# Two changes of DMA layout and queue in a two-layer scan kernel: 8-KB runs for two groups' intermediate, and the last phase's output stores on one queue

## The chip, the cores and the metric

The kernel runs on one core of a Trainium2 chip. The metric is the device time of one execution in microseconds (us), lower is better. The engines are PE (matmul), DVE (vector), ACT (scalar), POOL (general purpose) and SP, which does nothing here but issue DMAs. Both SP and ACT issue DMAs, each on a queue of its own; the profile calls SP's queue q1 and ACT's q10. ACT also computes, and it works its list in order: while it issues a DMA, or waits to, it doesn't compute.

## The reference

The input x has 32 images of 48 channels, 64 rows and 128 columns (fp32). Each of two layers normalises x over 16 groups of channels, then runs four scans over the picture (down and up over the rows, right and left over the columns), and adds the result to x:

```python
def step(w, b):
    def f(carry, inp):
        nxt = inp + _conv1d(carry, w, b)   # 5 taps along the other axis, 48 -> 48 channels
        return (nxt, nxt)
    return f
...
x = x + _L0_conv_ref(_gn(x), ...)
x = x + _L1_conv_ref(_gn(x), ...)
```

Every step of a scan needs the one before it, so the 64 rows are walked down and up and the 128 columns right and left, one after the other.

## The kernel before

**Tiling.** The 32 images are four groups of 8 (`GB`). A step is nine 128-wide matmuls and three additions on DVE that put a row (or column) in place. The chain of these steps is the kernel; all else is arranged around it.

**Phases.** `PHASES` lists twelve: for each layer the rows of groups 0, 1, 2 and 3, then the columns of groups 0 and 1 together (pair 0) and of 2 and 3 (pair 1). Phases 6 to 9 are the rows of layer 1, of which 8 and 9 (`JOINED`) share steps with the phase before; phase 10 and phase 11 are its columns. Phase 11 is the last one.

**Units.** In a column phase the picture is cut into four quarters of its columns (j), and each quarter into six units of 128 partitions x 2048 numbers (8 KB on each partition, 1 MB in all). The scan to the left finishes the quarters in the order 3, 2, 1, 0. What follows for each unit in phase 11 is written in `plan_cols`: `load_residual` brings the layer's input for the unit from `mid`, on ACT's queue; `add_residual` adds it (on POOL); `permute_unit` brings the eight 256-wide parts into the order of the output (three copies on POOL, five on ACT); `store_result` sends it to the output. For quarter 0, which is ready only when the scan ends, `last_results` does the same with the addition on DVE and the copies on ACT, POOL and DVE (3, 3, 2). Six tiles take the residuals in turn: a tile is loaded again when its unit's stores have landed.

**The intermediate.** `mid` (`source[1]`, one tensor in DRAM for each group) holds layer 0's result. It is written in phases 4 and 5 by `keep_result`, unit by unit (on SP's queue), read row by row in phases 6 to 9 by `take_rows` (SP's queue, runs of 32 numbers, 128 bytes), and read again unit by unit in phases 10 and 11 by `load_residual`. `by_quarter` gives the row view, `by_unit` the unit view. Its layout is [quarter, line, partition, 256]: the eight 1-KB lines of one partition of a unit lie 384 KB apart.

**The stores.** The output's rows of a quarter are 32 numbers long, so every output store of a column phase moves 128-byte runs. A unit is stored in three or four pieces (`pieces`), because 48 channels don't divide 128 partitions: 384, 384 and 256 KB, or 128, 384, 384 and 128 KB. In phase 11 the pieces alternate between SP's queue and ACT's; in the other phases all are on SP's.

**What sets the order.** `at(t, ...)` puts every piece of work on an agenda with a time in steps; `in_order` ties the instructions of each engine to that order. SP's list in phase 11 also has the six reads that bring back the units of quarter 0 which were spilled to DRAM (`spill_unit`); the scan needs them when it comes to quarter 0.

Of the kernel before, what the change touches and what calls it, by code (L numbers as in the profile page):

```python
# [29 lines left out]
F32 = mybir.dt.float32  # L30
# [3 lines left out]
C = 48  # L34
# [8 lines left out]
E8 = 8  # L43
FULL = 128
NG = E8 * C // FULL
NQ = 4
# [31 lines left out]
def weight_runs():  # L78
# [24 lines left out]
PHASES = (  # L103
    ("rows", 0, 0),
    ("rows", 0, 1),
    ("rows", 0, 2),
    ("rows", 0, 3),
    ("cols", 0, 0),
    ("cols", 0, 1),
    ("rows", 1, 0),  # L110
    ("rows", 1, 1),
# [10 lines left out]
def kernel(  # L122
# [8 lines left out]
    nc = tc.nc  # L131
    B, _, H, W = x.shape
    NK = W // E8
    NH = H // E8
# [4 lines left out]
    LINE = E8 * RUN  # L139
    UNIT = NH * LINE  # L140
    SLOT = 2 * NG * UNIT
    HALF = H // 2
    NGRP = B // GB
# [11 lines left out]
    dram = ctx.enter_context(tc.tile_pool(name="dram", bufs=1, space=bass.MemoryType.DRAM))  # L155
# [35 lines left out]
    def kept(name):  # L191
# [3 lines left out]
            for g in range(NGRP)  # L195
        ]

    source = [
        [
            dram.tile([E8 * NQ, C, UNIT], F32, tag=f"xin{g}", name=f"xin{g}")  # L200
# [2 lines left out]
            for g in range(NGRP)  # L203
        ],
        [
            dram.tile([NQ, NH, E8 * C, LINE], F32, tag=f"mid{g}", name=f"mid{g}")
            for g in range(NGRP)
        ],
    ]
# [53 lines left out]
    def by_quarter(t, e, h0, h1, q):  # L263


        t = t[q].rearrange("a (i c) (e n) -> e c (a i) n", i=E8, e=E8)
        return t[e, :, h0:h1]

    def by_unit(t, o, j):


        at = [(o * FULL, 0, FULL)]
        if o == NG - 1:
            at = [(6 * C, 0, 2 * C), (5 * C + C // 3, 2 * C, FULL)]
        t = t[j].rearrange("a m n -> m a n")
        return [(t[r : r + p1 - p0], p0, p1) for r, p0, p1 in at]

    def by_line(t):
# [18 lines left out]
    def dma(dst, src, queue=None):  # L297
        (queue or nc.sync).dma_start(dst, src)
# [21 lines left out]
    def pieces(o):  # L320
        return [(e, c0, c1, p0) for e, c0, c1, g, p0 in PIECES if g == o]
# [444 lines left out]
    def take_rows(k, h0, h1, o):  # L766

        _, layer, g = PHASES[k]
        turned = h1 - h0 > E8 and place(k, h0) > place(k, h0 + E8)
        if turned:  # L770
            for h in range(h0, h1, E8):
                take_rows(k, h, h + E8, o)
            return
        view = rows_at(k, h0, h1)
        for e, c0, c1, p0 in pieces(o):
            here = view[p0 : p0 + c1 - c0, o]
            for q in range(NQ):
                dma(
                    here[:, :, q * RUN : (q + 1) * RUN],
                    by_quarter(source[layer][g], e, h0, h1, q)[c0:c1],  # L780
                )
# [50 lines left out]
    def load_residual(k, j, i, nat):  # L832
        _, layer, pair = PHASES[k]
        o, half = UNITS[i]
        t = source[layer][2 * pair + half]
        if layer:
            for there, p0, p1 in by_unit(t, o, j):
                dma(by_line(nat)[p0:p1], there, nc.scalar)
        else:
            for e, c0, c1, p0 in pieces(o):  # L840
                here = nat[p0 : p0 + c1 - c0]
                if pair or half:
                    dma(here, x_by_col(t, e, j)[c0:c1])
                else:
                    dma(by_line(here), natural_col(t, e, j)[c0:c1])
# [6 lines left out]
    def keep_result(k, j, i):  # L852
        _, layer, pair = PHASES[k]
        o, half = UNITS[i]
        for there, p0, p1 in by_unit(source[1][2 * pair + half], o, j):
            dma(there, by_line(quarter(k, j)[:, half, o])[p0:p1])
# [17 lines left out]
    def in_output(j, g, e):  # L874


        t = out[g * GB : (g + 1) * GB].rearrange("b c (a e) w -> e (c a) b w", e=E8)
        return t[e, :, :, j * WQ : (j + 1) * WQ]

    def store_result(k, j, i, perm):  # L880
        pair = PHASES[k][2]
        o, half = UNITS[i]
        for n, (e, c0, c1, p0) in enumerate(pieces(o)):
            dst = in_output(j, 2 * pair + half, e)[c0 * NH : c1 * NH]
            src = perm[p0 : p0 + c1 - c0].rearrange("p (a b n) -> p a b n", a=NH, b=GB)
            queue = nc.scalar if n % 2 and k == len(PHASES) - 1 else nc.sync
            dma(dst.rearrange("(c a) b n -> c a b n", a=NH), src, queue)

    def hold_result(j, i, perm):
        o, half = UNITS[i]  # L890
# [225 lines left out]
    def plan_cols(k, t0, prev):  # L1116
# [32 lines left out]
        for u, (t, j, i) in enumerate(direct):  # L1149
            nat = tiles[u % n]  # L1150
            o, half = UNITS[i]
            if u < n:
                at(left + 16, load_residual, k, j, i, nat)
            if layer == 0:
                if u >= n:
                    at(max(direct[u - n][0] + 3, t - 21), load_residual, k, j, i, nat)
                at(t, add_residual, k, j, i, nat)
                at(t + 4, keep_result, k, j, i)
                unit = quarter(k, j)[:, half, o]
                if half == 0:  # L1160
                    for b in range(GB):
                        at(t + 5 + b, stats[0].take, j, o, unit, b)
                else:
                    at(t + 1, stats[1].take, j, o, unit)
            else:

                at(t, add_residual, k, j, i, nat)
                at(t + 2.5, permute_unit, k, j, i, nat, (nc.gpsimd, nc.scalar, nc.scalar))
                if final or j not in HELD:
                    at(t + 4.5, store_result, k, j, i, nat)  # L1170
                else:
                    at(t + 4.5, hold_result, j, i, nat)
                if final and j == 1:
                    at(t + 4.7, load_residual, k, 0, i, last_tiles(k)[i])

                if u >= 2 and u - 2 + n < len(direct):
                    at(t + 4.6, load_residual, k, *direct[u - 2 + n][1:], tiles[(u - 2) % n])
# [17 lines left out]
    def last_results(k):  # L1195

        for i, nat in enumerate(last_tiles(k)):
            perm = (*(stage[:, n] for n in range(4)), *spare_tiles)[i]
            add_residual(k, 0, i, nat, nc.vector)
            permute_unit(k, 0, i, perm, (nc.scalar, nc.gpsimd, nc.vector))  # L1200
            store_result(k, 0, i, perm)
# [3 lines left out]
    for k, (kind, *_) in enumerate(PHASES):  # L1205
        n = (H if kind == "rows" else W) - 1
# [283 lines left out]
```

## Time and profile before

| | |
|---|---|
| three runs, us | 4108.45, 4110.68, 4172.64; median 4110.68 |
| the profiled execution | 4108.49 us, its span (first to last instruction) 4106.8 us |
| PE busy | 4012.3 us, 98% of the span, mean granted clock 0.991 |
| DVE, ACT, POOL busy | 2078.8, 1306.9, 789.0 us |
| DMA | 681.57 MB in 2253898 packets, of which 2008848 are under 512 B |
| SP's queue, ACT's queue | 595.36 MB and 80.77 MB |

How to read it: the page's first part gives busy time by engine; the table of windows gives the same for stretches of the span, with the share of time in which the 16 DMA engines had packets and the GB/s. Packets of two queues can overlap, so that share can pass 1. The timeline lists an engine's instructions in order, with "ACTq" or "SPq" for the issue of a DMA; the time of such a row is the time the issuing took, not the transfer's. In a row of the timeline the bracket says how long the engine stood idle before and what ended it. The page's own chain of what ended last is one instruction long here (0.54 us) and tells nothing.

### The profile page before, as it was taken

Reading aid. Unit: us, or ns where it says so; the run is one execution under the profiler, and the core shown is the slowest. Engines: PE = TensorE matmul, PEld = TensorE weight load, DVE = VectorE, ACT = ScalarE, POOL = GpSimd, SP = SyncE. Lnnn points to the kernel's source line nnn. Section 1 sums busy time; section 2 is a strip of 40 time slices with the busy share of each in tenths; the row PEclk is TensorE's granted clock in tenths of the full one; section 3 lists DMA queues with packets and bytes.
Section 4 is the critical chain, followed back from the end, with each engine's and each line's share of the span. In section 5 each row is a group of like instructions: output and inputs, shape, how many; then the busy total and the mean of one; then the engine's idle time right before and its main releaser. Section 6 shows DMA issues by size and latency. Waiting matters only on the chain. (4 is left out here: it accounts for less than half of the span.)

```text
span 4106.8 us, 85201 instructions
## 1 busy us (share of the span) xinstructions
PE 4012.3 (98%) x34360; PEld 3927.0 (96%) x34360; DVE 2078.8 (51%) x6137; ACT 1306.9 (32%) x2628; POOL 789.0 (19%) x672
## 2 busy tenths in 40 slices
PE   6999999999999999999999999999999999999994
PEld 5999999999999999999999998888999999999994
DVE  6454454544444567546655443333444444444444
ACT  4557466430000355003773633434000002300122
POOL 5631303100000243002411000000000025610353
PEclk9999999999999999999999999999999999999997
DMA  9898897967993499804996965666698039999799
GB/s 299 220 223 185 245 189 218 171 108 97 147 181 60 141 245 288 193 2 155 242 161 143 142 102 96 101 108 104 103 166 202 1 77 245 299 251 155 147 234 196
DMA packets 2253898, 681.57 MB, mean 166 GB/s; under 512 B 2008848, under 2 KB 2206656, under 8 KB 2231232
## 3 DMA queue, kind: packets, MB, share of 16 engines
q1 hardware_dynamic: 2117568, 595.36, 70.3%
q10 hardware_dynamic: 135936, 80.77, 8.2%
q8 instruction: 270, 4.42, 0.5%
q14 instruction: 124, 1.02, 0.1%
HBM read 399.11 MB, written 295.93 MB: 169 GB/s over the span
## 5 line engine op out<-in xcount | busy, mean ns | idle before, releaser
L850 POOL TENSOR_TENSOR arena<-arena 128x2048 f32<-128x2048 f32 x80 | 362.5, 4547 | 1714.3 <-PE step_00l L915 521.3
L790 ACT ACTIVATE arena<-arena,offsetr,scaler 128x128 f32<-128x128 f32 (+1 forms) x576 | 345.2, 688 | 348.8 <-DMA arena<-mid 322.5
L648 ACT ACTIVATE early<-arena 128x256 f32<-128x256 f32 x192 | 129.7, 676 | 837.0 <-POOL arena L850 830.6
L790 ACT ACTIVATE arena<-arena,offset,scale 128x256 f32<-128x256 f32 (+2 forms) x360 | 249.0, 787 | 91.8 <-DMA arena<-xin 81.6
L709 POOL COPY arena<-arena 128x256 f32<-128x256 f32 x340 | 201.0, 653 | 383.7 <-DMA arena<-in_x 230.2
L915 PE MATMUL step_01r<-arena,early 128*128 128x128 f32 x2286 | 249.8, 272 | 0.0
L915 PE MATMUL step_11r<-arena,early 128*128 128x128 f32 x2286 | 249.2, 272 | 0.0
L915 PEld LDWEIGHTS step_11r<-arena,early 128*128 128x128 f32 x2286 | 248.7, 184 | 0.4 <-DVE arena L929 0.3
L915 PEld LDWEIGHTS step_01r<-arena,early 128*128 128x128 f32 x2286 | 248.9, 184 | 0.2
L915 PE MATMUL step_00r<-arena,early 128*128 128x128 f32 x2286 | 248.8, 272 | 0.0
L915 PEld LDWEIGHTS step_00r<-arena,early 128*128 128x128 f32 x2286 | 248.5, 184 | 0.2 <-DVE arena L929 0.2
L915 PE MATMUL step_10l<-arena,wleft 128*128 128x128 f32 x2286 | 248.5, 272 | 0.0
L915 PE MATMUL step_11l<-arena,wleft 128*128 128x128 f32 x2286 | 248.5, 272 | 0.0
L915 PE MATMUL step_00l<-arena,wleft 128*128 128x128 f32 x2286 | 248.4, 272 | 0.0
L915 PE MATMUL step_01l<-arena,wleft 128*128 128x128 f32 x2286 | 248.4, 272 | 0.0
L915 PE MATMUL step_10r<-arena,early 128*128 128x128 f32 x2286 | 248.4, 272 | 0.0
L915 PEld LDWEIGHTS step_10l<-arena,wleft 128*128 128x128 f32 x2286 | 248.4, 184 | 0.0
L915 PEld LDWEIGHTS step_11l<-arena,wleft 128*128 128x128 f32 x2286 | 248.4, 184 | 0.0
L915 PEld LDWEIGHTS step_00l<-arena,wleft 128*128 128x128 f32 x2286 | 248.4, 184 | 0.0
L915 PEld LDWEIGHTS step_01l<-arena,wleft 128*128 128x128 f32 x2286 | 248.4, 184 | 0.0
L915 PEld LDWEIGHTS step_10r<-arena,early 128*128 128x128 f32 x2286 | 248.4, 184 | 0.0
L872 ACT COPY arena<-arena 128x256 f32<-128x256 f32 x172 | 99.6, 656 | 366.6 <-POOL arena L850 234.7
(545 smaller groups left out, 6870.1 us busy)
## 6 DMA issues: line engine op xcount, KB each, us to landing
xin<-arena SPq DMA_DIRECT2D x94, 512.0 KB, 4.5
arena<-in_x SPq DMA_DIRECT2D x18, 2048.0 KB, 10.5
upa<-arena SPq DMA_DIRECT2D x192, 192.0 KB, 3.8
arena<-upa SPq DMA_DIRECT2D x96, 384.0 KB, 9.9
arena<-xin SPq DMA_DIRECT2D x96, 384.0 KB, 10.6
upb<-arena SPq DMA_DIRECT2D x192, 192.0 KB, 3.9
arena<-upb SPq DMA_DIRECT2D x96, 384.0 KB, 10.9
arena<-xin SPq DMA_DIRECT2D x174, 192.0 KB, 4.2
```

The costliest lines, as they stand in the source:

```text
L648: nc.scalar.activation(junk[:, 0:n], view[:, b], AF.Identity, accum_out=self.sum[:, i, j : j + 1])
L709: copy(dst[:, r, q], src[:, r0 + r, q])
L790: nc.scalar.activation(args[0], args[0], AF.Identity, bias=args[2], scale=args[1])
L850: eng.tensor_tensor(unit, unit, nat, ALU.add)
L872: copy(by_w(perm)[:, a], src[:, a])
L915: nc.tensor.matmul(part(turn(whole(ps[o]))[0:m], -s), weights[:, i, at : at + m], part(turn(src(i)), s), start=seen[o] == 1, stop=seen[o] ...
```

## The change

1. For groups 2 and 3 (`by_partition`) the layout of `mid` becomes [quarter, partition, 2048]: the eight lines of a partition lie one behind the other, 8 KB in one run, and a unit of 128 partitions is 1 MB in one piece (for the third unit of a half, whose partitions are held in two parts, 768 and 256 KB). Unit writes (phase 5) and unit reads (phase 11) then move 8-KB runs in place of 1-KB ones. The row reads of phases 8 and 9 keep their 128-byte runs, in the same number of DMAs; from one channel to the next it is 8 KB where it was 1 KB. Groups 0 and 1 stay as they were.
2. In phase 11 all pieces of a unit's store are issued on SP's queue, in the same order and the same sizes; ACT's list there has the residual loads and its copies only.

```diff
+    def by_partition(g):
+
+        return g >= NGRP - 2
+
...
         [
-            dram.tile([NQ, NH, E8 * C, LINE], F32, tag=f"mid{g}", name=f"mid{g}")
+            dram.tile(
+                [NQ, E8 * C, UNIT] if by_partition(g) else [NQ, NH, E8 * C, LINE],
+                F32,
+                tag=f"mid{g}",
+                name=f"mid{g}",
+            )
             for g in range(NGRP)
         ],
...
     def by_quarter(t, e, h0, h1, q):
 
 
+        if len(t.shape) == 3:
+            t = t[q].rearrange("(i c) (a e n) -> e a c i n", i=E8, a=NH, e=E8)
+            return t[e, h0 // E8, :, h0 % E8 : h0 % E8 + h1 - h0]
         t = t[q].rearrange("a (i c) (e n) -> e c (a i) n", i=E8, e=E8)
         return t[e, :, h0:h1]
...
-        t = t[j].rearrange("a m n -> m a n")
+        t = t[j].rearrange("m (a n) -> m a n", a=NH) if len(t.shape) == 3 else t[j].rearrange("a m n -> m a n")
         return [(t[r : r + p1 - p0], p0, p1) for r, p0, p1 in at]
...
     def store_result(k, j, i, perm):
         pair = PHASES[k][2]
         o, half = UNITS[i]
-        for n, (e, c0, c1, p0) in enumerate(pieces(o)):
+        for e, c0, c1, p0 in pieces(o):
             dst = in_output(j, 2 * pair + half, e)[c0 * NH : c1 * NH]
             src = perm[p0 : p0 + c1 - c0].rearrange("p (a b n) -> p a b n", a=NH, b=GB)
-            queue = nc.scalar if n % 2 and k == len(PHASES) - 1 else nc.sync
-            dma(dst.rearrange("(c a) b n -> c a b n", a=NH), src, queue)
+            dma(dst.rearrange("(c a) b n -> c a b n", a=NH), src)
```

## The prediction

> **What bounds the kernel now.** I read the page first, then the stage table (busy time by window), PE's waits, the timeline of the end, and the DMA view of single stretches.
>
> ```profile
> span 4106.8 us, 85201 instructions
> ...
> PE step_00d L915 <- DVE arena L929: 0.7, 1, 0.7
> ...
> PE step_10d L915 <- DVE arena L929: 0.2, 1, 0.2
> ```
>
> The last two rows are the longest and the shortest of the five waits that PE has between 130 and 4051 us. The stage table says the same (columns: length; busy time of PE, PEld, DVE, ACT, POOL; granted clock; DMA share; GB/s):
>
> ```profile
> 130.00:1392.00 1262.00, 1260.50 (x11504) 1259.51 (x11503) 622.96 (x1979) 452.33 (x908) 209.94 (x302) 1.00 0.81 163
> 1392.00:2400.00 1008.00, 1007.78 (x9229) 1005.57 (x9228) 602.77 (x1792) 465.98 (x994) 221.22 (x75) 1.00 0.77 179
> 2400.00:2870.00 470.00, 470.00 (x2422) 409.81 (x2422) 178.57 (x407) 192.53 (x368) 1.01 (x2) 1.00 0.63 99
> 2870.00:3864.00 994.00, 994.00 (x8858) 984.78 (x8857) 481.04 (x1479) 73.90 (x130) 152.68 (x97) 1.00 0.75 164
> 3864.00:4050.00 186.00, 185.95 (x1712) 185.76 (x1710) 91.44 (x286) 49.21 (x85) 113.80 (x72) 1.00 1.18 220
> 4050.00:4107.00 57.00, 0.00 (x0) 0.00 (x0) 25.12 (x19) 13.31 (x23) 12.73 (x18) 0.52 1.30 170
> ```
>
> The results of the last phase come in four quarters of six units (first to last in order of time); the last is ready when PE ends. From 130 to 4050 us PE is never without work. What the edit does there costs or gains nothing, as long as no operand of a scan comes late. Only the last 57 us are open: PE has ended, and DVE, ACT and POOL together work 51 us in them. The DMA share is 1.30 (two queues' packets overlap, so it passes 1), and already 1.18 in the 186 us before. So the tail is a DMA backlog that began when the last column phase's results started to leave, at 3864 us. The end of the program, by rows:
>
> ```profile
> 4052.66 2.12 POOL L872 COPY arena<-arena 128x256 f32<-128x256 f32 x3 [21.54 <-ACT early L872]
> 4054.07 6.75 ACTq L298 DMA_DIRECT2D arena<-mid  x2
> 4060.86 1.75 ACT L872 COPY arena<-arena 128x256 f32<-128x256 f32 x3 [7.51 <-issue]
> 4062.67 24.38 SPq L298 DMA_DIRECT2D out<-arena  x8
> 4065.17 5.00 ACTq L298 DMA_DIRECT2D out<-arena  x1
> 4070.27 1.74 ACT L872 COPY arena<-arena 128x256 f32<-128x256 f32 x3 [5.18 <-DVE arena L850]
> 4072.08 7.33 ACTq L298 DMA_DIRECT2D out<-arena  x2
> 4074.63 2.12 POOL L872 COPY early<-arena 128x256 f32<-128x256 f32 x3 [2.27 <-issue]
> 4088.85 14.19 SPq L298 DMA_DIRECT2D out<-early  x4
> ```
>
> POOL's copies of the first unit end at 4054.8, but ACT's begin at 4060.86, because ACT was 6.75 us in issuing two loads. So the first store of the last quarter goes out only at 4062.67. POOL has finished all six units by 4076.75; the last store is issued 26 us later (4088.85 + 14.19 = 4103.0), and the span ends 3.8 us after that.
>
> **The change part by part.** Where the order moves: ACT, at the last unit of the third quarter and the tail. Before:
>
> ```order
> L872 COPY early<-arena 128x256 x5
> L298 DMA out<-early 384x8x32
> L298 DMA arena<-mid_87 96x8x256
> L298 DMA arena<-mid_87 32x8x256
> L872 COPY arena<-arena 128x256 x3
> L298 DMA out<-arena 384x8x32
> ```
>
> Now, from the same place to the end:
>
> ```order
> L884 COPY early<-arena 128x256 x5
> L310 DMA arena<-mid_87 96x2048
> L310 DMA arena<-mid_87 32x2048
> L884 COPY arena<-arena 128x256 x12
> L884 COPY early<-arena 128x256 x6
> ```
>
> ACT has no store left; its 18 tail copies stand in one row, and the loads' runs are 2048 numbers (8 KB) where they were 256 (1 KB). SP takes the stores over. The first two units of the last quarter on SP, before:
>
> ```order
> L298 DMA out<-arena 384x8x32
> L298 DMA out<-arena 256x8x32
> L298 DMA out<-arena 384x8x32
> L298 DMA out<-arena 256x8x32
> L298 DMA out<-arena 128x8x32
> ```
>
> Now:
>
> ```order
> L310 DMA out<-arena 384x8x32 x2
> L310 DMA out<-arena 256x8x32
> L310 DMA out<-arena 384x8x32 x2
> L310 DMA out<-arena 256x8x32
> L310 DMA out<-arena 128x8x32
> ```
>
> Every piece is on SP, in the same sizes (128-byte runs). A unit is 128 x 8 KB = 1.049 MB; the phase stores 24 of them, and six are 6.29 MB.
>
> The rates come from these windows, same columns:
>
> ```profile
> 20.00:50.00 30.00, 29.99 (x118) 18.06 (x118) 28.12 (x51) 17.88 (x35) 21.97 (x47) 1.00 1.02 416
> 780.00:870.00 90.00, 90.00 (x823) 90.00 (x822) 43.82 (x137) 70.66 (x95) 0.00 (x0) 1.00 0.94 146
> 3120.00:3140.00 20.00, 20.00 (x186) 20.00 (x185) 9.79 (x32) 0.00 (x0) 0.00 (x0) 1.00 1.01 382
> 3320.00:3330.00 10.00, 10.00 (x95) 10.00 (x94) 5.00 (x16) 0.00 (x0) 0.00 (x0) 1.00 1.08 352
> 3690.00:3800.00 110.00, 110.00 (x1014) 110.00 (x1014) 54.27 (x169) 0.00 (x0) 0.00 (x0) 1.00 1.04 154
> 4074.00:4084.00 10.00, 0.00 (x0) 0.00 (x0) 2.06 (x3) 1.73 (x3) 2.12 (x3) 0.50 1.35 157
> 4084.00:4094.00 10.00, 0.00 (x0) 0.00 (x0) 0.00 (x0) 3.46 (x6) 0.00 (x0) 0.50 1.41 174
> 4094.00:4104.00 10.00, 0.00 (x0) 0.00 (x0) 0.00 (x0) 0.00 (x0) 0.00 (x0) 0.50 1.19 145
> ```
>
> (a) Residual loads. In 3320:3330 nothing but 1-KB loads of mid run: 352 GB/s, 2.98 us a unit. Loads of 8-KB runs from a mid laid out so are in no row. The nearest is 3120:3140, spill writes and column loads in 8-KB runs: 382 GB/s, 2.75 us. How many units are loaded inside the backlog:
>
> ```profile
> L298 ACTq DMA_DIRECT2D arena<-mid x16: 387/1582/7256, 3890.1 to 4059.7; - x16
> L298 ACTq DMA_DIRECT2D early<-mid x8: 579/2606/8000, 3934.9 to 4015.2; - x8
> ...
> DMA to landing us min/median/max: 6.8/10.5/16.2
> ```
>
> 24 DMAs, 18 units (six in two pieces). 18 x (2.98 - 2.75) = **-4.1 us**. Bounds: 0, if only bytes count, and -8.3 with the 416 GB/s that the input loads reach at 20:50 (2.52 us a unit).
>
> (b) The last six units' stores, 6.29 MB. Two queues now: the mean of the last three windows is 158.7 GB/s, 39.6 us. One queue: 3690:3800, where SP alone stores held results to the output in the same 128-byte runs, 154 GB/s, 40.8 us. **+1.2 us**. Bounds: 0, and +3.5 at the 146 GB/s of 780:870, the slowest long stretch of 128-byte runs on one queue.
>
> The Trainium skill speaks on this ("DMA: Bandwidth & Descriptors", section "Issuing engines are not separate DMA queues"): DMAs from any issuer share the same 16 DMA engines, so a second issuer saves the sequencer's time and gives no bandwidth. By that the term is 0, and the sum would be 1.2 us lower; the rows give the second queue 3%.
>
> (c) The 18 units before, 18.87 MB: the same 3% would be 3.6 us. But the loads still keep the second queue in use for part of that time; I take half, **+1.8 us**, bounds 0 and +3.6.
>
> (d) ACT. Its stores' issues go (5.00 and 7.33 us in the rows above), and so does its lag: the first store can leave at 4054.8 instead of 4062.67. At most -7.9 us; least 0, because the DMA engines were not idle meanwhile (share 1.30 over the whole tail). Near the latter: **-2 us**.
>
> Sum: -4.1 + 1.2 + 1.8 - 2 = -3.1. The profiled execution took 4108.49 us, 1.7 us more than its span, and 2.2 us less than the median of the three runs (4110.68). So span 4103.7 and time **4105.4 us**. The floor: stores from 4054.8, 40.8 us of them, 3.8 us to the end: 4099.4, time 4101.1.
>
> SP's spill reads of the first quarter now queue behind whole units. Their row and the row of SP's stores (both count, min/median/max ns of an issue, first and last start):
>
> ```profile
> L298 SPq DMA_DIRECT2D out<-arena x32: 590/2188/6660, 3871.6 to 4085.6; - x32
> ...
> L298 SPq DMA_DIRECT2D arena<-spill x6: 1592/4226/8192, 3875.7 to 3933.5; - x6
> ```
>
> The stores that come over from ACT are 427 of 1024 KB a unit: 2.6 MB, 17 us at 154 GB/s, so the last spill read goes out at 3951 at the latest. It is wanted by the scan of the last quarter, 62 us before 4050. Late by 37 us more, it would stop PE.
>
> The writes of groups 2 and 3 (phase 5, inside 1392:2400) become 8-KB runs. PE covers them; without that cover 48 units at the same 0.23 us would be worth 11 us. Their row reads in phases 8 and 9 keep their 128-byte runs, with 8 KB from channel to channel instead of 1 KB. I cost that at nothing: the share there is 0.63, and the reads at 780:870 have just that pitch and still make 146 GB/s at share 0.94.
>
> **The rivals.** *A, slower: the store queue starves beside the loads.* A ring of 128-byte packets shares each DMA engine with a ring of 8-KB packets. Two rows of the DMA view at 4064:4107 show what SP's queue got beside ACT's:
>
> ```profile
> q1 hardware_dynamic: 28864, 3.67, 68.3%
> q10 hardware_dynamic: 21167, 3.16, 59.9%
> ```
>
> That is 3.67 MB in 43 us, 85 GB/s, for SP. If all stores have that while loads are in flight, a quarter takes 6.29 / 0.085 = 74 us, where the scan delivers one in 62 (186 us for three). From 3871.6 three of them and 16.5 us of spill reads end at 4110; then come 40.8 us at the full rate and 3.8: span 4154, time **4156**. It decides when the lone queue falls under 6.29 MB / 62 us = 101 GB/s. Against it: in the first quarter of the phase before, SP stored while ACT loaded and held, and got this in 10 us (3400:3410):
>
> ```profile
> q1 hardware_dynamic: 8096, 1.10, 70.7%
> q10 hardware_dynamic: 1040, 1.05, 30.5%
> ```
>
> About 104 GB/s, just enough. The same page of the Trainium skill ("Queues, rings and completion order") has each DMA engine take turns between queues by packet; with 8-KB against 128-byte runs that speaks for A, and no run here shows it for these two sizes.
>
> *B, slower by over 2%: the row reads.* If an 8-KB pitch makes them slow, PE waits in phases 8 and 9. The DMA view of 2400:2870 has:
>
> ```profile
> arena<-mid SPq DMA_DIRECT2D x368, 48.0 KB, 2.1
> arena<-mid SPq DMA_DIRECT2D x124, 32.0 KB, 1.9
> arena<-mid SPq DMA_DIRECT2D x122, 16.0 KB, 1.9
> ```
>
> 24.1 MB, 157 us at 154 GB/s, while 0.37 x 470 = 174 us are free. Twice as dear is hidden; three times adds 140 us (**4248**). Against it: 780:870.
>
> *C, to the floor:* the 8-KB loads cost 2.52 us and ACT's lag is all real: **4101**. *D, the layout does nothing* (b and c alone, +3.0): **4111.5**; the order shows merged runs, which speaks against it.
>
> **How the numbers follow.** The forecast, 4102 to 4112, has 0.58; C and a little under 0.12; A, in full or in part, 0.22; D 0.03; B 0.04; anything faster by over 2% (4028, before PE ends) 0.01. A's greater part lies below 4122, since the two rings were seen to share. Range 4097 to 4122: the bounds (-16 cut by the floor, +7) and half of A. Faster by over 2% (about what a measurement can tell from no change) 0.01, slower by over 2% 0.05 (B, and a worse A), within 0.94.
>
> **What would show it.** PE ends at 4050 again, with no wait above 1 us after 130. ACT's tail copies follow DVE's adds without issue gaps; the tail's first store leaves near 4055 to 4060; the tail's GB/s is about 154. I am wrong if PE waits in phases 8 or 9, if the third quarter's stores still go out after 4065 (A), or if the 18 loads' landing (median 10.5 us now) does not fall.

## The result, and the profile after

| | before | after |
|---|---|---|
| median of 4 runs, us | 4109.57 (4105.98 to 4172.64) | 4141.8 (4139.03 to 4144.48) |
| span of the profiled execution, us | 4106.8 | 4140.2 |
| ratio after / before | | 1.0081, 95% interval 1.0062 to 1.0101 |

The change makes the kernel 0.8% slower, some 33 us by the ratio. That is within 2%, as forecast, but on the other side of the forecast, and outside the range of 4097 to 4122. (The run of 4172.64 is a slow one, 1.6% above the fastest of the same kernel, and is not in the ratio.)

**Up to the end of the scans nothing moved.** PE's waits from 130 to 4055 us in the profile after:

```profile
PE step_02u L926 <- DVE arena L940: 0.3, 1, 0.3
...
PE step_01u L926 <- DVE arena L940: 0.3, 1, 0.3
```

The stage table after, with the same columns as in the prediction:

```profile
2400.00:2870.00 470.00, 470.00 (x2432) 410.09 (x2431) 178.45 (x408) 190.87 (x366) 1.01 (x2) 1.00 0.62 99
...
3864.00:4050.00 186.00, 186.00 (x1715) 186.00 (x1714) 91.54 (x286) 51.89 (x90) 113.95 (x72) 1.00 0.90 204
...
4050.00:4140.00 90.00, 2.12 (x20) 1.92 (x18) 24.02 (x22) 10.44 (x18) 21.34 (x18) 0.54 0.84 140
```

The rows with the new 8-KB pitch (2400:2870) are read at the same 99 GB/s and the same share, 0.62 against 0.63. PE is busy all through the last column phase and ends at 4052, 2 us later than before. What differs stands in the last two columns of the last two rows: the DMA share was 1.18 and 1.30 and is 0.90 and 0.84, the rate was 220 and 170 GB/s and is 204 and 140. The same bytes take longer, first beside the loads and then alone.

How much each stretch is worth can be worked out from these rows. By 4050 both kernels have asked for the six spilled units and 17 of the 18 residual units, 24.1 MB. Before moved 220 x 186 = 40.9 MB in the stretch, so 16.8 MB of it were stores; after moved 204 x 186 = 37.9 MB, so 13.8 MB were stores (74 GB/s over the 186 us, of which the first 10 are over before a store is issued). All 24 units are 25.2 MB. Before had 8.4 MB left at 4050 and 57 us to go, after has 11.4 MB left and 90 us to go. The 3.0 MB more, at 8.4 MB / 57 us = 147 GB/s, are 20 us; the lower rate of the tail, 11.4 MB / 90 us = 127 GB/s, makes the other 13.

**SP is never short of work.** SP's timeline after, from 3945 us on, and then the same of before from 3930 us:

```profile
3949.97 50.06 SPq L310 DMA_DIRECT2D out<-arena  x14
4000.14 25.25 SPq L310 DMA_DIRECT2D out<-early  x6
4025.51 53.01 SPq L310 DMA_DIRECT2D out<-arena  x14
4078.63 13.04 SPq L310 DMA_DIRECT2D out<-early  x6
4091.84 30.75 SPq L310 DMA_DIRECT2D out<-arena  x14
4122.75 13.42 SPq L310 DMA_DIRECT2D out<-early  x6
```

```profile
3935.25 35.95 SPq L298 DMA_DIRECT2D out<-arena  x8
3976.67 17.12 SPq L298 DMA_DIRECT2D out<-early  x4
3996.73 38.48 SPq L298 DMA_DIRECT2D out<-arena  x8
4043.82 14.24 SPq L298 DMA_DIRECT2D out<-early  x4
```

Fourteen stores from `arena` and six from `early` are one quarter. Before, SP ends a quarter after some 60 us and has gaps between the rows: the scan, which gives a quarter each 62 us, sets the pace. After, each row begins where the one before ends, and the quarter from 3949.97 to 4025.51 takes 75.5 us. An issue of a store takes 0.59 us at the least and 3.1 us in the middle (the row of them stands further below); I read the long ones as a queue that takes a new DMA only as it drains. The third quarter's stores still go out until 4091.7, and the last quarter, which has been ready since the 4050s, begins 29 us later than before (4062.67). Alone it then takes 4091.84 to 4136.2, 44.3 us of issue.

**The wait has moved to ACT.** ACT's timeline after, at the end (the bracket is the idle time before the row and what ended it):

```profile
4054.74 1.75 ACT L884 COPY arena<-arena 128x256 f32<-128x256 f32 x3 [10.26 <-DVE arena L862]
...
4063.45 1.73 ACT L884 COPY arena<-arena 128x256 f32<-128x256 f32 x3 [6.97 <-DMA out<-arena]
```

ACT's first copy of the tail begins 6 us sooner than before (4060.86), as forecast. But the copies after it need a tile, and tiles come free when stores have landed: ACT now waits for the DMA queue, 7 us at a time. Residual loads after (issue ns as min/median/max):

```profile
L310 ACTq DMA_DIRECT2D arena<-mid x16: 325/344/1497, 3883.8 to 4050.7; - x16
L310 ACTq DMA_DIRECT2D early<-mid x8: 308/325/331, 3936.8 to 4030.4; - x8
...
DMA to landing us min/median/max: 5.8/8.3/14.1
```

Issuing such a load costs ACT 0.34 us where it cost 1.58, and it lands in 8.3 us where it took 10.5. Both looked like the layout's doing; the runs below show that they are mostly the queue's. Either way they buy nothing, because at the end the stores are late and not the residuals.

**What one queue looks like.** Six microseconds of stores alone, in 40 slices of 0.15 us, one queue (after, DMA view of 4085:4091), and then two queues (before, the same stretch):

```profile
DMA  9997499999999999999999999999785410499999
GB/s 217 211 187 114 63 172 207 207 206 193 184 161 152 151 175 204 172 166 158 151 146 158 164 164 169 169 160 138 122 131 99 65 27 2 81 180 179 179 180 180
```

```profile
DMA  9999999999999999999999999999999999999999
GB/s 185 186 186 186 193 193 201 195 185 189 189 182 185 182 187 178 181 173 181 176 172 174 172 149 154 147 150 170 185 186 181 174 173 174 171 169 166 160 164 165
DMA packets 8345, 1.06 MB, mean 177 GB/s; under 512 B 8345, under 2 KB 8345, under 8 KB 8345
...
q1 hardware_dynamic: 4725, 0.60, 82.3%
q10 hardware_dynamic: 3620, 0.46, 62.3%
```

With one queue there are holes: the rate falls from 187 to 63 and from 131 to 2 GB/s and is back after 0.3 to 0.8 us. Each lies where one store ends and the next begins. Not every such place has one: the second hole comes 4.4 us after the first, which at 154 GB/s is 0.67 MB, a piece of 384 KB and one of 256, and between these two no hole is seen. With two queues the share never leaves 9. I read it so that q10's packets fill the hole while q1 changes over. That reading is theory G below.

### The profile page after: what moved, and what is told of

Read it like the earlier page. It is cut to its first block, busy times and chain, and to the rows that moved or that the text cites. A ratio compares the mean times of both kernels' runs of the same rounds, so it can differ in the third digit from the quotient of the medians.

```text
span 4140.2 us, 85182 instructions
## 1 busy us (share of the span) xinstructions
PE 4014.2 (97%) x34360; PEld 3928.4 (95%) x34360; DVE 2074.9 (50%) x6137; ACT 1306.3 (32%) x2628; POOL 797.8 (19%) x672
## 4 chain that ended last, share of the span: by engine, by line
PE 91%; SPq 5%; DMA 2%; POOL 1%; issue 0%; DVE 0%; POOLq 0%
PE step_01r L926 6%; PE step_11r L926 6%; PE step_00r L926 6%; PE step_10l L926 6%; PE step_10r L926 6%; PE step_01l L926 6%; PE step_00l L926 6%; SPq L310 5%; PE step_11l L926 3%; PE step_10d L926 3%; PE step_10u L926 3%; PE step_11d L926 3%; PE step_13u L926 3%; PE step_01d L926 3%; PE step_03u L926 3%; PE step_02d L926 3%
```

## The experiments

All medians in us; "before" is the kernel before, run beside each on the same chip. The three kernels without loads ran once each.

| run | median | ratio to before, 95% interval | profiled span |
|---|---|---|---|
| layout only | 4106.9 | 0.9994 [0.9985, 1.0003] | 4105.2 |
| one queue only | 4139.41 | 1.0073 [1.0061, 1.0086] | 4138.8 |
| change with 2-KB runs | 4143.95 | 1.0084 [1.0068, 1.0099] | 4140.1 |
| change, last quarter only on one queue | 4113.35 | 1.0015 [1.0005, 1.0025] | 4111.0 |
| change, smallest pieces on ACT | 4133.85 | 1.0064 [1.0049, 1.0079] | 4131.4 |
| change, pieces cut | 4159.63 | 1.0122 [1.0102, 1.0142] | 4157.7 |
| change, loads on SP too | 4139.54 | 1.0073 [1.0056, 1.009] | 4136.4 |
| layout, two store queues, loads on SP | 4126.98 | 1.0043 [1.0028, 1.0058] | 4124.4 |
| layout, two store queues, loads on POOL | 4110.7 | 1.0005 [0.9996, 1.0014] | 4109.4 |
| layout, units alternate | 4114.28 | 1.0013 [1.0004, 1.0022] | 4112.3 |
| layout, balanced alternation | 4109.79 | 1.0004 [0.9995, 1.0012] | 4108.4 |
| change without loads | 4103.36 (one run) | | 4101.6 |
| change without loads, pieces cut | 4108.87 (one run) | | 4107.2 |
| before without loads | 4111.9 (one run) | | 4110.2 |

### Which half of the change

Theory Q says that the lost time is the lone store queue's, whatever the layout; R that it is the layout's; QR that it needs both, 8-KB load packets beside 128-byte store packets (rival A as the prediction put it). Layout only, from the kernel after:

```diff
-        for e, c0, c1, p0 in pieces(o):
+        for n, (e, c0, c1, p0) in enumerate(pieces(o)):
...
+            queue = nc.scalar if n % 2 and k == len(PHASES) - 1 else nc.sync
```

> Only the layout of groups 2 and 3 (8-KB runs); the last phase's stores alternate between SP and ACT as before. Theory Q (a lone queue of 128-byte stores leaves the DMA engines partly idle beside loads in the other queue): the second store queue is back, so 4098 to 4109 us, no slower than before. Theory R (the 8-KB loads push the 128-byte stores aside, in whichever queue these are): 4125 to 4145. If it takes both together (theory QR): 4098 to 4109 here and about the time of before in the run with one queue only.

One queue only, from the kernel before:

```diff
-        for n, (e, c0, c1, p0) in enumerate(pieces(o)):
+        for e, c0, c1, p0 in pieces(o):
...
-            queue = nc.scalar if n % 2 and k == len(PHASES) - 1 else nc.sync
-            dma(dst.rearrange("(c a) b n -> c a b n", a=NH), src, queue)
+            dma(dst.rearrange("(c a) b n -> c a b n", a=NH), src)
```

> Only the stores on one queue; the layout stays in 1-KB lines. Theory Q: 4132 to 4150 us, all of the loss. Theory R: 4103 to 4115, since 1-KB loads let the stores through (SP had 104 GB/s beside such loads in the phase before). Theory QR: 4103 to 4115 too, with the layout-only run also near before.

A layout between the two, runs of 2 KB, from the kernel after (the views `by_quarter`, `by_unit` and `by_line` follow it):

```diff
+    JOIN = 2
...
-                [NQ, E8 * C, UNIT] if by_partition(g) else [NQ, NH, E8 * C, LINE],
+                [NQ, NH // JOIN, E8 * C, JOIN * LINE] if by_partition(g) else [NQ, NH, E8 * C, LINE],
```

> The changed kernel with two lines of 1 KB joined instead of eight: groups 2 and 3 move 2-KB runs, stores on one queue. Theory Q: 4135 to 4150, the run's length doesn't matter. Theories R and QR: between, nearer to 1 KB: 4108 to 4125.

Measured: 4106.9, 4139.41 and 4143.95. The layout alone can't be told from no change. The queue alone has nearly all of the loss with the old 1-KB runs, and 2-KB runs change nothing. R and QR fall, Q stands. The stage table of the one-queue run:

```profile
3864.00:4050.00 186.00, 184.67 (x1700) 184.48 (x1698) 92.35 (x286) 52.06 (x90) 112.71 (x72) 1.00 0.95 206
4064.00:4094.00 30.00, 0.00 (x0) 0.00 (x0) 13.17 (x12) 5.88 (x11) 15.04 (x11) 0.50 0.81 133
```

and of the layout-only run:

```profile
3864.00:4050.00 186.00, 186.00 (x1714) 186.00 (x1713) 91.50 (x286) 49.84 (x87) 113.91 (x72) 1.00 1.16 221
4064.00:4094.00 30.00, 0.00 (x0) 0.00 (x0) 12.53 (x9) 6.95 (x12) 6.79 (x10) 0.50 1.39 167
```

206 and 133 GB/s against 221 and 167: the two rates of after and of before, with the layouts changed over. The residual loads of the one-queue run, with the old 1-KB runs:

```profile
L298 ACTq DMA_DIRECT2D arena<-mid x16: 320/385/4630, 3880.3 to 4048.2; - x16
...
DMA to landing us min/median/max: 5.9/8.8/14.9
```

They are issued in 0.39 us and land in 8.8, nearly as in the change. In the layout-only run the medians are 2.08 us and 9.6. So it is ACT's queue without stores, not the 8-KB runs, that made loads quick to issue; the runs are worth 0.5 to 0.9 us of landing.

### How much is the tail, how much the quarters before it

Without the residual loads after the first six units, first on the change and then on the kernel before, the same two lines:

```diff
-                if final and j == 1:
+                if False:
...
-                if u >= 2 and u - 2 + n < len(direct):
+                if not final and u >= 2 and u - 2 + n < len(direct):
```

> The changed kernel without the residual loads of the last phase after the first six units (the additions then use what stands in the tiles; the result of three quarters is left wrong by that). All theories: the stores alone keep pace, so the backlog at the end of PE is small: the first store of the last quarter by 4060, the last quarter's stores in 44 us (two of the six units at 8.8 us, four at 6.65, as in the changed kernel's tail), span 4100 to 4106. If the lone queue is slow even without loads, the span is over 4115 and both theories fall.

> The kernel before (1-KB layout, stores on two queues) without the residual loads of the last phase after the first six units (three quarters of the results are left wrong by that). It gives the pace of the stores alone on two queues, beside 46.9 us for the last quarter on one queue without loads. Theory P (a store DMA holds its queue about 2.2 us whatever its size from 128 to 384 KB, so a second queue works in its shadow): last quarter in 38 to 41 us, the engines' own rate, span 4093 to 4097. Theory L (only the loads' turns make one queue lag): as on one queue, 45 to 47 us, span 4100 to 4103.

Measured: 4103.36 for one queue. SP's timeline of that run at its end:

```profile
4053.59 30.32 SPq L310 DMA_DIRECT2D out<-arena  x14
4084.08 13.45 SPq L310 DMA_DIRECT2D out<-early  x6
```

With no loads beside them the three quarters' stores keep up on one queue, and the last quarter begins at 4053.59. But it takes 43.9 us of issue, almost as long as in the change (44.3). So one queue has two prices: the last quarter's own, and a backlog, which needs the loads.

Two queues without loads came out slower than one: 4111.9. SP's waits there from 4040 us on:

```profile
SPq L298 <- DMA out<-arena: 27.4, 3, 22.1
```

SP stood still for 22 us until a store had landed. The trace has that store: ACT issued it for the last quarter at 4059.26, it landed at 4063.53, and SP's store of the third quarter went on at 4063.54. Both report their landing to the same semaphore. So the wait comes from the program's order and its semaphores, and this run says nothing on the rate of two queues.

To split the loss directly, two queues for three quarters and one for the last, on the layout of the change:

```diff
+            queue = nc.scalar if n % 2 and k == len(PHASES) - 1 and j else nc.sync
```

> Layout of the change; stores on two queues in the last phase except for the last quarter, whose stores are all on SP. It parts the loss: the tail's own share is the 47 us of one queue against 40 on two, so 4110 to 4116 if the backlog of the three quarters before makes the rest (all theories that put the loss beside the loads); 4130 or more if the tail makes it.

Measured: 4113.35, 6.5 us above layout only (6.7 when each is taken against the kernel before on its own chip) and 28 us under the change. Its last quarter:

```profile
4061.18 32.31 SPq L310 DMA_DIRECT2D out<-arena  x14
4093.64 13.30 SPq L310 DMA_DIRECT2D out<-early  x6
```

It begins at 4061.18 (4060.81 in the layout-only run) and is issued in 45.8 us against 40.7. So some 6 us are the last quarter on one queue, and some 28 us are the three quarters before it, stored beside the loads.

### What makes one queue slower

P is the theory of a fixed price for each store DMA, about 2.2 us; S puts the loss on the small pieces, B on bytes alone and L on the loads' turns. Each 384-KB piece was cut into 256 and 128 KB, without loads; 32 store DMAs a quarter in place of 20:

```diff
+        todo = []
...
+            cut = 2 * C // 3 if c1 - c0 == C and k == len(PHASES) - 1 else c1 - c0
+            todo += [(e, c, min(c + cut, c1), p0 + c - c0) for c in range(c0, c1, cut)]
+        for e, c0, c1, p0 in todo:
```

> The one-queue kernel without loads (as e4, three quarters of the results left wrong), each 384-KB piece of a store cut in two of 256 and 128 KB: 32 store DMAs a quarter in place of 20, the same packets. Theory P: a unit of three pieces goes from 6.65 us to 11, one of four from 8.8 to 13.2; a quarter takes 70 us and the span is about 4175. Theory S (only pieces of 16 partitions are slow, 2.0 us for 128 KB): a quarter takes about 62, span 4120 to 4145. Theory B (bytes alone): no change, 4100 to 4104.

Measured: 4108.87, 5.6 us more than the same without cuts (profiled spans, 4107.2 against 4101.6), below the ranges of P and S and above that of B. If all of it belongs to the twelve more DMAs of the last quarter, each costs 0.47 us. These are single runs on two chips, and runs of one kernel differ by 5 us and more; SP's issue of that quarter, which does not hang on the rest of the run, grew by 3.9 us (47.8 against 43.9), 0.32 for each. Either is far from 2.2. Then only the 128-KB pieces on ACT, on the change:

```diff
+            queue = nc.scalar if c1 - c0 == C // 3 and k == len(PHASES) - 1 else nc.sync
```

> The changed kernel with only the 128-KB pieces (two in each four-piece unit, 8% of the bytes) on ACT's queue in the last phase. Theories P and S: SP's list loses about 2 us for each, 8 us a quarter, and the backlog that grows beside the loads is nearly gone: 4104 to 4116. Theory B: 8% of 44 us, 3.6 us a quarter: 4122 to 4132. Theory L: little, 4130 to 4140.

Measured: 4133.85, 8 us less than the change: in L's range, and too slow for P, S and B. What the small pieces cost can be read in the change's own trace. DMA view of 4114:4120, which begins with one of them:

```profile
DMA  2003444444446999866889999999999886423211
GB/s 43 9 0 67 79 85 81 82 84 81 86 81 112 177 153 151 143 119 118 139 144 157 160 168 166 193 201 197 172 166 160 141 134 107 73 47 50 31 26 19
```

A hole of 0.4 us, then 1.3 us in which the 16 engines are 0.4 busy and move 82 GB/s, then the next pieces at full share. A 128-KB piece by itself keeps the engines less than half busy, and on a lone queue nothing else fills the rest. The change's stage table in its last quarter, cut by the kind of unit that is landing (two of three pieces, the two of four, two of three again):

```profile
4095.00:4108.00 13.00, 0.00 (x0) 0.00 (x0) 1.01 (x2) 1.59 (x3) 2.09 (x3) 0.50 0.97 155
4108.00:4126.00 18.00, 0.00 (x0) 0.00 (x0) 0.00 (x0) 0.00 (x0) 0.00 (x0) 0.50 0.73 123
4126.00:4139.00 13.00, 0.00 (x0) 0.00 (x0) 0.00 (x0) 0.00 (x0) 0.00 (x0) 0.50 0.89 145
```

The share is 0.73 where the small pieces are and 0.89 or more elsewhere. Theory G takes this up: a lone queue loses time at each DMA's end (and with each piece too small for all engines), and any second store queue's packets fill the holes. Its rival X: two queues, one with loads and one with stores, hinder each other, so that one common queue would be well again. G says that cuts with loads make it worse still and that a common queue does not help; X says the opposite. The cuts of above on the change itself:

> The changed kernel, all loads in, each 384-KB piece of a store in the last phase cut in 256 and 128 KB (32 store DMAs a quarter for 20, same packets, one queue). Without loads the same cut moved the end by 5.6 us (4101.6 to 4107.2), 0.47 us for each of the twelve more. Theory G (the lone queue has a gap where one DMA ends and the next begins, and nothing fills it): the backlog takes the 5.6 us in each of four quarters, 4158 to 4168. Theory X (only the loads crossing from the other queue hold the stores up): the tail's 5.6 us alone, 4144 to 4150.

And the loads put on SP, on the change:

```diff
-                dma(by_line(nat)[p0:p1], there, nc.scalar)
+                dma(by_line(nat)[p0:p1], there, nc.sync if k == len(PHASES) - 1 else nc.scalar)
```

> The changed kernel with the residual loads of the last phase on SP's queue too, so everything is in one queue and ACT issues nothing. Theory X: nothing crosses any more; a load costs its own 2.75 to 3.2 us instead of 5.2, and with 18 loads the time falls to 4103 to 4120. Theory G: loads and stores follow each other with gaps as before, 4128 to 4145.

Measured: 4159.63 and 4139.54, both in G's ranges; X falls. With the loads on SP no turn is taken between queues any more, and the loss is all there; SP does not stand still for a landing in that run, its waits from 3864 to 4125 us are for other engines alone. The 48 more DMAs of the cuts cost 17.8 us by the medians, 0.37 each. With the cuts the stage table has:

```profile
3864.00:4050.00 186.00, 185.70 (x1710) 185.51 (x1709) 91.53 (x286) 51.90 (x90) 113.84 (x72) 1.00 0.85 197
4064.00:4094.00 30.00, 0.00 (x0) 0.00 (x0) 16.34 (x12) 6.98 (x12) 10.20 (x12) 0.50 0.71 118
```

Share and rate of a lone queue fall with the number of DMAs: 0.71 and 118 GB/s with the cuts, 0.81 and 133 without (the one-queue run above). Two queues have 1.39 and 167 (layout only).

### Other ways to use the queues

Two store queues, and the loads on SP, the edit of the run before on the layout-only kernel:

> 8-KB layout, stores on two queues, residual loads on SP's queue instead of ACT's. Theory G: two store queues fill each other's gaps wherever the loads are, 4098 to 4110; if ACT, without the loads' issues, is the gain, the lower half of that. Theory X: the loads cross ACT's share of the stores only, 4100 to 4115.

Measured: 4126.98, outside what either theory gave. SP's waits in it from 3864 us on say why:

```profile
SPq L310 <- DMA out<-arena: 41.9, 8, 14.8
SPq L310 <- DMA out<-early: 15.4, 5, 8.9
```

A load needs its tile free, so it waits until stores have landed, and on SP everything behind it waits too, 57 us in all. It is an effect of the order on SP and says nothing against G. Loads on POOL's queue, a third one, on the layout-only kernel:

```diff
+                dma(by_line(nat)[p0:p1], there, nc.gpsimd if k == len(PHASES) - 1 else nc.scalar)
```

> 8-KB layout, stores on SP's and ACT's queues, residual loads issued by POOL, a third queue. If a third queue fills what gaps are left: 4096 to 4104. If the end is the DMA engines' own rate: 4104 to 4108. If issuing costs POOL time that its additions need: over 4110.

Measured: 4110.7, the same as before: a third queue gains nothing that can be measured. Two queues that share the stores in another way, whole units in turn, which leaves each queue's own row of DMAs as it is and only puts another beside it:

```diff
+            queue = nc.scalar if i % 2 and k == len(PHASES) - 1 else nc.sync
```

> 8-KB layout; in the last phase all pieces of a unit stay in one queue, units alternate between SP and ACT. Theory G (a queue has a gap of some 0.7 us between two DMAs, and another queue's packets fill it): any second queue of stores will do, 4104 to 4116. If the pieces of one unit must go side by side (a unit's store has to be short for its tile to come free): 4120 to 4135.

Measured: 4114.28, in G's range and 27.5 us less than the change. Its stage table:

```profile
3864.00:4050.00 186.00, 186.00 (x1715) 186.00 (x1714) 91.56 (x287) 51.45 (x90) 113.88 (x72) 1.00 1.11 218
4064.00:4094.00 30.00, 0.00 (x0) 0.00 (x0) 12.29 (x9) 6.75 (x12) 6.54 (x10) 0.50 1.21 170
```

218 and 170 GB/s, the rates of the kernel before. And pieces in turn with a change of the first queue from unit to unit, so that both queues get the same bytes:

```diff
+            queue = nc.scalar if (n + i) % 2 and k == len(PHASES) - 1 else nc.sync
```

> 8-KB layout; pieces alternate between the queues, and which queue takes the first piece alternates from unit to unit, so each queue has half the bytes (SP had 58%). Theory G: the queue that ends last ends sooner, 4099 to 4106 against 4106.9 with the old alternation. If the end is the DMA engines' own rate: 4104 to 4108.

Measured: 4109.79, the same as before, and slower than G or the rate alone would have it. How the stores are shared out matters little, that they are shared at all is worth 27 to 35 us. No version here beats the kernel before by more than the interval. In these versions, with two store queues and the loads not on SP, the DMA share of 4064:4094 is 1.2 to 1.4 and the rate 164 to 171 GB/s, whichever way the stores are shared out: few holes are left to fill there.

## Why the prediction was wrong, point by point

**(a), the residual loads, -4.1, and (d), ACT's freedom, -2.** Layout only, which has (a) without the rest, gives 0.9994 [0.9985, 1.0003]: 1.4 us less at the median (4106.9 against 4108.3 on the same chip), which cannot be told from nothing; 0 was the lower bound of (a). For (d), ACT's first tail copy did start at 4054.74 for 4060.86. (d) came to nothing because the stores that the copies feed could not leave: the tail's first store went out at 4091.84, not between 4055 and 4060.

**(b), the last quarter on one queue, +1.2, at most +3.5.** Measured +6.5 (4113.35 against 4106.9). I took the one queue's rate, 154 GB/s, from 3690:3800, where `held` goes to the output. It was the wrong neighbour: the last quarter takes 45.8 us of issue on one queue, 137 GB/s. The DMA share in the last quarter of the change is 0.73 to 0.97, as shown above, against 1.04 in the row I used. `held` is in DRAM and the last quarter comes from the tiles; whether that makes the difference was not tested. The trace of before has no stretch in which SP alone stores from the tiles with nothing beside it, and the range should have gone lower than the slowest row at hand.

**(c), the 18 units before it, +1.8, at most +3.6.** This is the step that failed: measured some +28. I took 3% of the stores' own time, as if the stage had room for it, and even halved that, because the loads "still keep the second queue in use". The stage has no room. Three quarters on two queues are 3 x 40.7 us of stores, and the 25.2 MB of loads and spill reads beside them are 66 us at the 382 GB/s of the prediction: an estimate of 188 us, where the scan gives 186. On one queue it is 3 x 44.3 + 66 = 199, and all that is above 186 ends up behind PE's end. The measured three quarters, 3873.8 to 4091.84, are 218 us. So a lone queue's own 3.6 to 5.1 us in each quarter (44.3 and 45.8 against 40.7) make 11 to 15 of the 28; the rest is lost beside the loads. Loads on the other queue don't stand in for a second store queue: for some time in the middle of a load no store moves at all. The change's DMA view of 3968:3970:

```profile
DMA packets 61, 0.50 MB, mean 250 GB/s; under 512 B 0, under 2 KB 0, under 8 KB 0
...
q10 hardware_dynamic: 61, 0.50, 90.6%
```

There is no row for q1 in these 2 us, though SP's list was full. The kernel before has the same with 1-KB runs (3962.5:3965):

```profile
DMA packets 728, 0.69 MB, mean 276 GB/s; under 512 B 61, under 2 KB 728, under 8 KB 728
...
q10 hardware_dynamic: 728, 0.69, 90.0%
```

The Trainium skill has this in "DMA: Bandwidth & Descriptors", section "Queues, rings and completion order": a DMA engine takes turns between the queues it has work for, and drains a whole packet, 9 to 17 descriptors as a rule and 64 at most, before it switches. The traces agree as far as they go: in both stretches the loads have the engines to themselves for 2 us and more, with 1-KB as with 8-KB runs (1024 runs of 1 KB are 64 for each of the 16 engines, an estimate that fits the largest packet and not the usual one), and the size of the runs does not matter (4139.41, 4143.95 and 4141.8 with 1, 2 and 8 KB). The turns as such are not the loss, since loads in the stores' own queue cost as much (4139.54); it is that the loads' time comes on top of a store time with holes. The lone queue then gets 83 GB/s in the second quarter (6.29 MB in 75.5 us) where it needed 101.

The section "Issuing engines are not separate DMA queues" of the same page of the Trainium skill, by which a second issuer saves issue time only, was cited for (b) as the lower price. The runs go against so low a price for these 128-byte stores: a second store queue is worth 27 to 35 us here (4114.28, 4109.79 and 4106.9 against 4141.8), at the same bytes and the same sizes of the DMAs. Whether the holes are time of the issuing SP, which that section would allow, no run here separates.

**The rivals.** A had the place, the direction and what to look for (stores of the third quarter after 4065) right, and its deciding point, 101 GB/s for the lone queue, was missed: 83 GB/s in the second quarter. That this is near the 85 it was priced with is luck, because the 85 were SP's part while another store queue worked beside it. Its size, 4156, was too high, because it added 16.5 us of spill reads to three quarters of 74 us. The stores of the change by their start:

```profile
L310 SPq DMA_DIRECT2D out<-arena x56: 590/3125/13587, 3873.8 to 4119.4; - x56
```

The quarters begin at 3873.8, 3949.97, 4025.51 and 4091.84, so they take 76.2, 75.5 and 66.3 us: the one with the spill reads is less than 1 us longer than the next. Its cause, 8-KB against 128-byte packets, is not what decides. The evidence used against A, 104 GB/s in one window of 10 us (3400:3410), was too short to hold whole turns of loads, and the whole quarter around it, which was overlooked, says the opposite. SP's timeline before, the first and the last row of that quarter:

```profile
3374.17 6.08 SPq L298 DMA_DIRECT2D out<-arena  x3
...
3455.03 2.40 SPq L298 DMA_DIRECT2D arena<-spill  x1
```

In the column phase before the last one all stores are on SP already. Its first quarter, 20 stores and six spill reads, with 7.34 MB of ACT's loads and writes beside them, took SP from 3374.17 to 3457.43 without a gap. That is 83 us for what the scan of the last phase delivers in 62, and nearly the case that the change makes of the last phase (76.2 us there). It spoke for A, which at 0.22 was underrated.

B is refuted (share 0.62, 99 GB/s, no wait of PE). C supposed a queue that keeps up. D had the layout right, which does nothing, but its time stood on (b) and (c).

**What was to show it.** PE's waits came as forecast and its end within 2 us. The loads' landing fell, but that sign came by luck: 8.3 us, where the old layout with ACT's queue free of stores has 8.8 and the new layout without that 9.6. The tail's rate of 154 GB/s was 140, the first store came 32 us late, and the third quarter's stores went on until 4091.7, which was named as the sign for A.

**What stays open.** What the loads add to a quarter on one queue can be read from the change's DMA view of 3949.97:4025.51:

```profile
q1 hardware_dynamic: 46920, 7.00, 55.2%
q10 hardware_dynamic: 1040, 7.34, 33.5%
```

These are seven loads on q10, and on q1 a spill read beside the stores: 8.4 MB, 22 us at 382 GB/s. They added 75.5 - 44.3 = 31 us. At the 250 and 276 GB/s of the two stretches shown above they would be 30 to 34 us (an estimate), so beside stores the loads themselves run slower; why they do is not shown. Nor are the holes all that a lone queue lacks: with the small pieces on ACT the share of 4064:4094 is 0.97, and the rate still 149 GB/s against 167 with two store queues. What makes the hole between two DMAs, and why some have none, was not tested either.

## What to carry to other kernels

Before putting all stores of a stage on one queue, look at the DMA share in short slices: here a lone queue of short-run stores had a share of 0.8 to 0.9 and holes between its DMAs, a second queue of stores filled them, and loads on another queue were no substitute. Price a queue by the sum of what it must move beside its neighbours against the pace at which work arrives (here 6.29 MB each 62 us), and not by its rate alone; a backlog of a few microseconds a quarter adds up at the end. A rate is taken from a row with the same source, destination and neighbours, over a whole round of the work and not over 10 us of it; where there is none the bound goes well beyond the nearest row.

## What the runs showed of the hardware

- A lone queue of 128-byte stores showed holes of 0.3 to 0.8 us where one DMA followed another, though not at every such place (4085:4091 of the change); each further cut of a piece cost 0.3 to 0.5 us (4107.2 against 4101.6 and 47.8 us of issue against 43.9 for 12 cuts in the last quarter, 4159.63 against 4141.8 for 48 cuts beside loads).
- A 128-KB store piece held the 16 DMA engines only 0.4 busy and moved 82 GB/s, where larger pieces moved mostly 150 to 200 (4114:4120 and 4085:4091 of the change).
- Loads in 1-KB, 2-KB and 8-KB runs made no difference to the time (4139.41, 4143.95 and 4141.8 on one queue; 0.9994 [0.9985, 1.0003] on two, 8 KB against 1). What made them quick to issue on ACT was a queue without stores: 0.39 us with 1-KB runs and 0.34 with 8-KB, against 1.58 and 2.08 with stores on the same queue.
- While a load of 1 MB was in its middle, the other queue's 128-byte stores moved nothing for 2 us and more (3968:3970 after, 3962.5:3965 before).
- Reading 128-byte runs at a pitch of 8 KB in place of 1 KB cost nothing: 99 GB/s and a share of 0.62 against 0.63.
